# A two-layer transformer block on one core: which engine adds in the first pass, and who orders the second layer

## The chip, the cores and the metric

The kernel runs on one core of one Trainium2 chip. The metric is the device time of one execution in microseconds (us); the result is compared as the median of several runs. The core has a matrix engine (TensorE, in the profile PE; its weight loads are PEld), VectorE (DVE), ScalarE (ACT), GpSimd (POOL), and SyncE (SP), which here only starts transfers (DMA). Every engine works through a queue of its own, strictly in the queue's order; semaphores hold an instruction back until what it reads is there and what it overwrites is no longer needed. TensorE writes its products to PSUM; everything else lies in SBUF or in HBM.

## The reference

Two layers over x of shape 8 x 256 x 512 (2048 tokens, 512 channels), all in float32. In each layer the normalized tokens go to an attention and to a feed-forward part, and both results are added to x.

```
x  = hidden_states                                  # (8, 256, 512)
xn = layernorm(x)
# layer 0, attention: 32 heads of 128, linear attention with decay
qkv    = silu(xn @ qkv_w.T)                          # 512 -> 3 * 4096
attn   = causal (q k^T * decay) v, per head          # scanned in blocks of 32
normed = norm_w * attn * rsqrt(mean(attn^2) + eps)   # over 4096
L0a    = (sigmoid(xn @ gate_w.T) * normed) @ out_w.T # 4096 -> 512
# layer 0, feed-forward: 16 experts, 2 chosen per token, and a shared one
L0f    = sum_e gate_e * ((silu(xn@w1+b1) * (xn@w2+b2)) @ w3 + b3) + shared(xn)
x  = x + L0a + L0f
xn = layernorm(x)
# layer 1, attention: one head of 128, softmax over 256 tokens
L1a = softmax(q k^T / sqrt(128)) v @ Wo + bo
# layer 1, feed-forward: 64 low-rank experts of rank 16, 16 chosen per token
G   = softmax over the 16 best of xn @ Wr.T          # (tokens, 64)
L1f = 2 * ((xn @ A) * G) @ B                         # 512 -> 1024 -> 512
out = x + L1a + L1f
```

## The kernel before

The 2048 tokens are four chunks of 512 (`CH`), each chunk two sequences of 256 (`S`). The program has four stages. The opening (0 to about 134 us) normalizes, computes the router and the shared expert. Two passes over the heads follow: the first (134 to 1240 us) for chunks 0 and 1, the second (to about 2406 us) for chunks 2 and 3. The second layer comes last, chunk by chunk (2406 to 2688 us).

**Seven products for eight.** The large matrix products are done by a scheme that multiplies two 2 x 2 block matrices with seven products p1 to p7 of sums of blocks, in place of eight. In the passes it is applied twice, one inside the other: an *outer product* (class `Outer`, one of seven in `ORDER`) takes one weight operand and one token operand, and computes its own product by seven inner ones. A pass goes over 8 groups of four heads (`g`), two halves of each (`h` = 0: q and k; `h` = 1: gate and v), and seven outer products: 112 outer products, 784 inner ones.

One outer product runs so (the loop over `plan`, L1500): p1 into a bank `ps_a`, p7 into `ps_e`, then p3 of the outer product *before*, then p6 (into the same `ps_a`), p4 (`ps_e`), p2 (`ps_b`), p5 (`ps_a`). In between, a running sum in a bank is taken out three times (`copied`, L1218: c1 after p1, c3 after p7, c2 after p6), and four results for the four quarters `q` of a tile are made from a bank and such a copy (`result`, L1227). Two banks `ps_a`, one `ps_e`, one `ps_b` are all there is, so a later product into a bank waits until it is taken out.

The four tiles `a`, `b`, `c`, `d` (named `c` in the profile) collect the outer products: p1 gives a; p2 gives b = a + product; p5 gives c = a + product; p3 gives d = c + product; p6, p4 are added to a, p7 to a and c. There are two ways to add such a running tile: *folded* (L1214), when the copy out of the bank is itself an addition on VectorE, `cp<-ps_a,c`; or apart, when ScalarE copies (`cp<-ps_a`, L1224), VectorE adds the bank to it, and GpSimd adds the tile afterwards (`c<-c`, `c<-c,r`). Before, the second pass folds (`self.u.i` is 1) and the first does not (0). In p7, the second pass adds the fourth result from the bank to c and to a on VectorE; the first copies it with ScalarE and lets GpSimd add it to c and VectorE to a. VectorE also does the first pass's other additions `a <- a + r` of p7 (`add_a`).

**Weight operands** (`weights`, L839). In the second pass all sums of weight blocks come ready from HBM. The first pass makes them while the outer product before runs, and stores them (`store`, issued by ScalarE). `outer_sum` (L849) makes the operand of p6, p5, p3 and p7 from the raw quarters, on 2 x 256 columns at a time (`w<-w 128x512`); p6's step makes p5's too, so it has four of them, p3 and p7 two each, and the others none: eight in each half of a group. `inner_sum` (L852) makes the four sums for the inner products, w7 = w1 - w0, w4 = w0 + w3, w5 = w4 - w1 and w6 = w2 - w5 (`w<-w 128x256`); the last on GpSimd, the rest on VectorE. The list `steps` says after which inner product of the running outer product each is issued.

Between the inner products smaller pieces of work are issued (`later`, `slot`): `silu` and `gate` (ScalarE, L975 to L982), scores, `attend` (the square of `ps_o` on ScalarE, its sums on GpSimd, `gT` on VectorE, L1031), the output product L1084 with its addition `acc<-ps_sc,acc`, and in the second pass the experts. Near the end of each pass, `combine` (L643, seven additions of `acc` on GpSimd) and `finish` (L649, VectorE) turn the sums of the chunks into the layer's result.

**Order.** In the two passes the queues of ScalarE, GpSimd and VectorE stand in the order of issue (`tc.manual_schedule`, L811). TensorE's and SyncE's are ordered by a planner. In the opening and in the second layer the planner orders all of them, but for instructions marked `keep_in_program_order`.

**Second layer** (the loop at L1633). For each chunk: `low_rank(0)` and `low_rank(2)` multiply the tokens by A, with the seven products in `seven` (L1552): p1, p2, p6, p7, p5, p3, p4, the bank copied by ScalarE (L1558) or added up by VectorE (`cp<-ps_b`, `cp<-ps_e`) and multiplied by the gates (`hg<-cp,spread_g`); then a third `seven` multiplies by B, adding `cp` to the output on GpSimd and the bank on VectorE, and writes the rows out. Dictionaries `fill1`, `fill2` and `fill` say what is issued behind each product. For the chunk itself: `turned` (transposes of the softmax, a copy `pT`), `weighed` (times v), `attended` (times Wo; `bo` is added on GpSimd, `spare<-spare,wob`). For the chunk after it: `gather` (GpSimd's indirect transfers of the experts' rows), `settle` (adds them, L629), for chunks 2 and 3 `finish`, then `stats` and `scaled` (the layer norm, L256 and L263), and in the third `seven` the transposes (L283), `route` with `choose` (the gates of the 64 experts, L710 to L720), `qk`, `softmax` (L755 to L764) and `gates`, whose result goes to HBM (`gd<-GT`) and comes back spread over the partitions (`spread_g<-gd`). Chunks 2 and 3 have their `combine` issued here too (`steps`, L1779). Chunk 0's share of this is done at the end of the second pass.

Of the kernel before, what the change touches and what calls it, by code (L numbers as in the profile page):

```python
# [73 lines left out]
def block_kernel(  # L74
# [24 lines left out]
    nc = tc.nc  # L99
# [438 lines left out]
    at = NTT * E  # L538
# [110 lines left out]
    def finish(i, r, ns=range(TPC), kept=lambda ins: ins):  # L649

        for n in ns:
            o = r[:, n, :].rearrange("p (h c) -> p h c", h=2)
            at = 2 * (n // 2)
            kept(
                nc.vector.scalar_tensor_tensor(
                    o, acc[i][:, at : at + 2, n % 2], all_rms[i][:, n : n + 1], o, ALU.mult, ALU.add
                )
            )
# [152 lines left out]
    with tc.tile_pool(name="attn", bufs=1) as attn, tc.manual_schedule(engines={mybir.EngineType.Activation, mybir.EngineType.Pool, mybir.EngineType.DVE}):  # L811
# [27 lines left out]
        def weights(i, g, h, p, steps):  # L839

            w = loaded[p].pop(0)
            y = w[:, 0:4]
            v = nc.vector
            pool = nc.gpsimd
            kept = ws[2 * g + h][p]
            if i == 0:
                latest[p] = y

                def outer_sum(f, o, a, b, n):  # L849
                    f(o[:, n : n + 2], a[:, n : n + 2], b[:, n : n + 2], v)  # L850

                def inner_sum(f, o, a_, b_):  # L852
                    f(w[:, o], w[:, a_], w[:, b_], pool if o == 6 else v)
                    if o == 6:
                        later(6, store)

                def store():
                    nc.scalar.dma_start(out=kept, in_=w[:, 4 if p in RAW else 1 : 8])

                outer = []  # L860
                if p == "p6":
                    w5 = loaded["p5"][0]
                    outer = [(add, w5, w5, w5[:, 4:8]), (sub, y, w5, y)]
                elif p == "p3":
                    outer = [(sub, y, y, latest["p6"])]
                elif p == "p7":
                    outer = [(sub, y, y, w[:, 4:8])]
                for n, when in ((0, "p1"), (2, "p7")):
                    steps += [(when, partial(outer_sum, *at, n)) for at in outer]
                steps += [  # L870
                    (when, partial(inner_sum, *at)) for when, at in (
                        ("p7", (sub, 7, 1, 0)), ("p6", (add, 4, 0, 3)), ("p6", (sub, 5, 4, 1)), ("p2", (sub, 6, 2, 5))
                    )
                ]
            return dict(zip(("p1", "p2", "p4", "p5", "p6", "p3", "p7"), (w[:, n] for n in range(1, 8))))
# [316 lines left out]
        class Outer:  # L1192
# [20 lines left out]

            def folded(self, q):  # L1214

                return self.u.i and (self.p, q) not in (("p4", 0), ("p4", 3)) and {"p2": "a", "p5": "a", "p6": "a", "p4": "a", "p3": "c"}.get(self.p)

            def copied(self, bank, q):  # L1218
                c = attn.tile([P, 512], FP, tag="cp", name="cp", bufs=5)
# [7 lines left out]
            def result(self, i, j, bank, c):  # L1227

                u, p, q = self.u, self.p, 2 * i + j
                pool = nc.gpsimd  # L1230
                a = u.tile(self.h, "a")[:, q]
                made, with_ = dict(
                    p1=("a", None), p2=("b", "a"), p5=("c", "a"), p3=("d", "c")
                ).get(p, (None, None))
                if made:
                    o = u.tile(self.h, made)[:, q]
                    if c is None and with_ is None:
                        nc.scalar.copy(o, bank)
                    elif c is None:
                        add(o, bank, u.tile(self.h, with_)[:, q])  # L1240
                    else:
                        add(o, bank, c)
                        if with_ and not self.folded(q):
                            add(o, o, u.tile(self.h, with_)[:, q], pool)
                elif p != "p7" and (c is None or self.folded(q)):
                    add(a, bank, a if c is None else c)
                elif p == "p7" and c is None and u.i:
                    c_ = u.tile(self.h, "c")[:, q]
                    add(c_, bank, c_)
                    add(a, bank, a)  # L1250
                else:
                    r = attn.tile([P, 512], FP, tag="sum", name="r", bufs=4)
                    if c is None:
                        nc.scalar.copy(r, bank)
                    else:
                        add(r, bank, c)
                    if p != "p7":
                        add(a, a, r, pool)
                    else:
                        c_ = u.tile(self.h, "c")[:, q]  # L1260
                        add(c_, c_, r, pool)

                        self.added.append(partial(add_a, a, r, pool if u.i else nc.vector))
                        if (i, j) == (1, 1):
                            for n in range(3):
                                later(n, self.added.pop(0)) if n else self.added.pop(0)()
                        elif (i, j) == (0, 1):
                            self.added.pop(0)()
                whole = dict(p2=("b", 0, 0), p3=("d", 0, 1), p7=("c", 1, 1), p4=("a", 1, 0)).get(p)
                if whole and (i, j) == (0, 1):  # L1270
                    Part(u, self.h, whole[1], whole[2], u.tile(self.h, whole[0])).begin()
# [228 lines left out]
        for n, (i, g, h, p) in enumerate(plan):  # L1500
            cur = outers[n]
            u = cur.u
# [126 lines left out]
        return x_  # L1629


    out_t = out.rearrange("(i t p) c -> i t p c", t=TPC, p=P)
    for i in range(NCH):  # L1633
        xc, yT = accs[i], xT[i]
# [74 lines left out]
        following = []  # L1709
        if i + 1 < NCH:  # L1710
# [1 line left out]
            for n in range(TOP):  # L1712
                gather(i + 1, n, following[1 + n])
        fill1 = {
            1: [],
            2: [partial(turned, 0)], 7: [partial(turned, 1)], 5: [partial(weighed, 0)], 3: [partial(weighed, 1)], 4: [],
        }
        fill2 = {k: [partial(attended, t)] for t, k in enumerate((2, 7, 5, 3))}
        fill2[4] = []
        if following:  # L1720
            settled[i + 1] = spare()
            whole = Normal(settled[i + 1], following[0])

            def stats(t):
                whole.stats(t, tc.keep_in_program_order)

            def scaled(t):
                tc.keep_in_program_order(whole.scaled(t))

            if i:  # L1730
                fill1[1].append(lambda: finish(i + 1, following[0], kept=tc.keep_in_program_order))
            for n, fill, k, ts in (
                (0, fill1, 3, (0, 1)), (0, fill1, 4, (2, 3)), (1, fill2, 2, (0, 1)), (1, fill2, 7, (2, 3)),
            ):
                fill[k].append(partial(settle, i + 1, n, following[0], following[1 + n], ts))
            fill2[7] += [partial(stats, 0), partial(stats, 1)]
            fill2[5] += [partial(stats, 2), partial(stats, 3), whole.root]
            fill2[3] += [partial(scaled, 0), partial(scaled, 1)]
            fill2[4] += [partial(scaled, 2), partial(scaled, 3)]
# [136 lines left out]
```

## Time and profile before

| | us |
|---|---|
| median of 3 runs | 2686.19 (2685.26 to 2689.57) |
| the profiled execution's own time | 2689.79 |
| its span, first to last instruction | 2688.1 |

| stage (us) | PE busy | PEld | DVE | ACT | POOL |
|---|---|---|---|---|---|
| opening, 0 to 134 | 121.0 | 69.6 | 101.5 | 51.4 | 82.1 |
| first pass, 134 to 1240 | 1083.4 | 971.5 | 872.1 | 427.1 | 776.2 |
| second pass, 1240 to 2406 | 1159.7 | 1035.5 | 707.8 | 312.8 | 501.1 |
| second layer, 2406 to 2688 | 267.0 | 216.2 | 177.3 | 49.0 | 66.8 |

The mean granted clock of TensorE is 0.994 of full. The profile was taken from one execution. A busy time counts the union of an engine's instructions; the ends of matmuls are modelled, so a busy TensorE may still be slowed, which shows in the distance from one start to the next. In a group's line stand the source line, engine and operation, output and inputs by the program's names, shapes, and the number of instructions; then the busy time and the mean of one in ns; then the time that the engine stood idle just before them, and for what. Additions all have line L103, since one helper issues them: they are told apart by the names of their tiles. In a line of the waits stand who waited for whom, and then the total, the number of times and the longest.

### The profile page before, as it was taken

To read this page: it belongs to the slowest core of one execution; us is meant where nothing else is said; L and a number is where in the kernel's file an instruction comes from. 1 tells how busy PE (TensorE), PEld (TensorE's weight loads), DVE (VectorE), ACT (ScalarE), POOL (GpSimd) and SP (SyncE) were. 2 spreads that over 40 slices of the span, in tenths; PEclk is the share of its full clock that TensorE was granted. 3 is DMA by queue.
4 is the path that set the end of the run, shared out by engine and by line. 5 is a ranking of instruction groups with operands and counts; after the bars stand their busy time and mean duration, and the time that the engine had idled before them with its cause. 6 is when DMAs were issued, how large, how long until landed. Compare 5 with 4: busy or idle time off the path is not lost. (4 is left out here: it accounts for less than half of the span.)

```text
span 2688.1 us, 38735 instructions
## 1 busy us (share of the span) xinstructions
PE 2631.1 (98%) x14218; PEld 2292.8 (85%) x14218; DVE 1858.7 (69%) x3161; ACT 840.3 (31%) x1233; POOL 1426.1 (53%) x1326
## 2 busy tenths in 40 slices
PE   8999999999999999999999999999999999999999
PEld 5578888888888888888989898888989898977777
DVE  8698777778787878766556565656666565757763
ACT  4234343434343434342322123222313132321121
POOL 7458686868686767574433435353433454463210
PEclk8999999999999999999999999999999999999999
DMA  6798686868686868695868676777768686634211
GB/s 251 290 384 307 234 299 227 299 234 300 233 299 234 307 231 306 227 332 206 299 244 281 219 290 237 268 268 249 261 234 282 236 310 223 223 102 145 79 42 65
DMA packets 163120, 655.62 MB, mean 244 GB/s; under 512 B 19776, under 2 KB 22336, under 8 KB 160960
## 3 DMA queue, kind: packets, MB, share of 16 engines
q1 hardware_dynamic: 125936, 499.16, 52.7%
q10 hardware_dynamic: 21024, 92.81, 8.5%
q0 software_dynamic: 15968, 61.13, 6.8%
q8 instruction: 115, 1.88, 0.3%
q14 instruction: 77, 0.63, 0.1%
HBM read 512.13 MB, written 143.78 MB: 244 GB/s over the span
## 5 line engine op out<-in xcount | busy, mean ns | idle before, releaser
L887 PE MATMUL ps_a<-xt,w 128*128 128x256 f32 x2688 | 717.5, 382 | 8.4 <-ACT cp L1224 4.1
L887 PEld LDWEIGHTS ps_a<-xt,w 128*128 128x128 f32 x2688 | 470.7, 191 | 65.7 <-issue 11.2
L103 POOL TENSOR_TENSOR c<-c,r 128x512 f32<-128x512 f32 x288 | 382.1, 1346 | 217.2 <-DVE r L103 217.0
L1084 PE MATMUL ps_sc<-wo,gT 128*128 128x256 f32 x1792 | 424.0, 380 | 3.2 <-ACT head L758 2.6
L1224 ACT COPY cp<-ps_a 128x512 f32<-128x512 f32 x304 | 177.5, 584 | 678.5 <-PE ps_a L887 586.3
L1084 PEld LDWEIGHTS ps_sc<-wo,gT 128*128 128x128 f32 x1792 | 334.3, 190 | 47.8 <-issue 5.0
L887 PE MATMUL ps_e<-xt,w 128*128 128x256 f32 x1344 | 366.2, 381 | 7.0 <-DVE c L103 6.5
L103 DVE TENSOR_TENSOR w<-w 128x256 f32<-128x256 f32 (+1 forms) x464 | 353.8, 771 | 5.4
L103 POOL TENSOR_TENSOR sums<-sums,sq 128x256 f32<-128x256 f32 x240 | 192.4, 802 | 304.5 <-ACT sq L1022 294.9
L887 PEld LDWEIGHTS ps_a<-w,xt 128*128 128x128 f32 x1792 | 270.5, 191 | 23.0
L887 PE MATMUL ps_a<-w,xt 128*128 128x128 f32 x1792 | 272.3, 275 | 0.0
L103 POOL TENSOR_TENSOR c<-c 128x512 f32<-128x512 f32 x144 | 191.4, 1339 | 146.5 <-DVE c L103 138.1
L887 PEld LDWEIGHTS ps_e<-xt,w 128*128 128x128 f32 x1344 | 232.1, 191 | 31.6 <-DVE c L103 8.0
L103 DVE TENSOR_TENSOR acc<-ps_sc,acc 128x512 f32<-128x512 f32 x196 | 134.6, 688 | 149.2 <-PE ps_sc L1084 149.0
L1031 DVE SCALAR_TENSOR_TENSOR gT<-ps_o,nw,c 128x256 f32<-128x256 f32 x256 | 112.0, 479 | 166.0 <-ACT sq L1022 137.9
L103 DVE TENSOR_TENSOR c<-ps_a,c 128x512 f32<-128x512 f32 x192 | 130.3, 686 | 97.8 <-PE ps_a L887 97.0
L887 PE MATMUL ps_b<-xt,w 128*128 128x256 f32 x672 | 182.1, 380 | 0.0
L103 DVE TENSOR_TENSOR s<-ps_sc,decay 128x384 f32<-128x384 f32 x256 | 140.1, 553 | 56.3 <-PE ps_sc L999 55.4
L103 POOL TENSOR_TENSOR gT<-gT 128x512 f32<-128x512 f32 x128 | 170.2, 1330 | 5.5 <-DVE gT L1031 3.0
L1022 ACT ACTIVATE sq<-ps_o 128x512 f32<-128x512 f32 x128 | 76.6, 599 | 301.3 <-PE ps_o L1012 277.5
L1011 PE MATMUL ps_o<-s,c 128*128 128x256 f32 x512 | 157.3, 389 | 8.9 <-DVE gT L1031 8.5
L998 PE MATMUL ps_sc<-c 128*128 128x256 f32 x512 | 152.6, 380 | 0.0
(293 smaller groups left out, 4288.1 us busy)
## 6 DMA issues: line engine op xcount, KB each, us to landing
xt<-xc SPq DMA_DIRECT2D x224, 896.0 KB
w<-in_w_att_dram SPq DMA_DIRECT2D x144, 512.0 KB
w<-in_w_att_dram SPq DMA_DIRECT2D x48, 384.0 KB
wo<-in_w_out_dram SPq DMA_DIRECT2D x56, 256.0 KB
decay<-dec SPq DMA_DIRECT2D x32, 384.0 KB
yd<-ye SPq DMA_DIRECT2D x36, 256.0 KB
wos<-wo ACTq DMA_DIRECT2D x32, 256.0 KB
wo<-wos SPq DMA_DIRECT2D x32, 256.0 KB
```

Source lines behind the costliest of these rows:

```text
L103: (eng or nc.vector).tensor_tensor(o, a, b, op)
L887: mm(o, a, b, start=(first and ty == 0), stop=True, skip_group_check=True)
L998: mm(p[:, 0:S], k[:, 0:P], q, start=True, stop=True)
L1011: mm(po[:, bass.ts(hh, S)], v[:, 0:P], s[:, 0:S], start=True, stop=False)
L1022: nc.scalar.activation(sq, po, AF.Square)
L1031: nc.vector.scalar_tensor_tensor(gT[:, h, :], po[:, bass.ts(h, S)], nw[:, n : n + 1], self.c[:, 2 * h + t, 0:S], ALU.mult, ALU.mult,)
L1084: mm(py[:, bass.ts(t, S)], self.O[l, p][:, hh, bass.ts(t, P)], self.wo[p][:, hh, :], start=(t == 0 and hh == 0), stop=(hh == 1), skip_grou ...
L1224: nc.scalar.copy(c, bank)
```

## The change

In the first pass: `outer_sum` goes from VectorE to GpSimd; for the outer products that have one (p6, p3, p7), `inner_sum`s are issued later (w7 after p4 in place of p7, w4 and w5 after p2 in place of p6, w6 after p5 in place of p2). `folded` holds in the first pass as in the second, so that the running tile is added by VectorE in the copy out of the bank; the fourth result of p7 is added from the bank on VectorE; the other `add_a` go to GpSimd. What is computed stays the same.

In the second layer: ScalarE, GpSimd and VectorE work in the order of issue. Both `turned` come one product earlier or more (after p1 and p2 of the first `seven`, in place of p2 and p7), and `finish` of the following chunk is issued in two parts, after p2 and p7, in place of one after p1.

```diff
--- before.py
+++ after.py
@@ -847,7 +847,7 @@
                 latest[p] = y
 
                 def outer_sum(f, o, a, b, n):
-                    f(o[:, n : n + 2], a[:, n : n + 2], b[:, n : n + 2], v)
+                    f(o[:, n : n + 2], a[:, n : n + 2], b[:, n : n + 2], pool)
 
                 def inner_sum(f, o, a_, b_):
                     f(w[:, o], w[:, a_], w[:, b_], pool if o == 6 else v)
@@ -867,9 +867,10 @@
                     outer = [(sub, y, y, w[:, 4:8])]
                 for n, when in ((0, "p1"), (2, "p7")):
                     steps += [(when, partial(outer_sum, *at, n)) for at in outer]
+                whens = ("p4", "p2", "p2", "p5") if outer else ("p7", "p6", "p6", "p2")
                 steps += [
-                    (when, partial(inner_sum, *at)) for when, at in (
-                        ("p7", (sub, 7, 1, 0)), ("p6", (add, 4, 0, 3)), ("p6", (sub, 5, 4, 1)), ("p2", (sub, 6, 2, 5))
+                    (when, partial(inner_sum, *at)) for when, at in zip(
+                        whens, ((sub, 7, 1, 0), (add, 4, 0, 3), (sub, 5, 4, 1), (sub, 6, 2, 5))
                     )
                 ]
             return dict(zip(("p1", "p2", "p4", "p5", "p6", "p3", "p7"), (w[:, n] for n in range(1, 8))))
@@ -1213,7 +1214,7 @@
 
             def folded(self, q):
 
-                return self.u.i and (self.p, q) not in (("p4", 0), ("p4", 3)) and {"p2": "a", "p5": "a", "p6": "a", "p4": "a", "p3": "c"}.get(self.p)
+                return (self.p, q) not in (("p4", 0), ("p4", 3)) and {"p2": "a", "p5": "a", "p6": "a", "p4": "a", "p3": "c"}.get(self.p)
 
             def copied(self, bank, q):
                 c = attn.tile([P, 512], FP, tag="cp", name="cp", bufs=5)
@@ -1244,7 +1245,7 @@
                             add(o, o, u.tile(self.h, with_)[:, q], pool)
                 elif p != "p7" and (c is None or self.folded(q)):
                     add(a, bank, a if c is None else c)
-                elif p == "p7" and c is None and u.i:
+                elif p == "p7" and c is None:
                     c_ = u.tile(self.h, "c")[:, q]
                     add(c_, bank, c_)
                     add(a, bank, a)
@@ -1260,7 +1261,7 @@
                         c_ = u.tile(self.h, "c")[:, q]
                         add(c_, c_, r, pool)
 
-                        self.added.append(partial(add_a, a, r, pool if u.i else nc.vector))
+                        self.added.append(partial(add_a, a, r, pool))
                         if (i, j) == (1, 1):
                             for n in range(3):
                                 later(n, self.added.pop(0)) if n else self.added.pop(0)()
@@ -1629,6 +1630,7 @@
         return x_
 
 
+    ctx.enter_context(tc.manual_schedule(engines={mybir.EngineType.Activation, mybir.EngineType.Pool, mybir.EngineType.DVE}))
     out_t = out.rearrange("(i t p) c -> i t p c", t=TPC, p=P)
     for i in range(NCH):
         xc, yT = accs[i], xT[i]
@@ -1712,8 +1714,8 @@
             for n in range(TOP):
                 gather(i + 1, n, following[1 + n])
         fill1 = {
-            1: [],
-            2: [partial(turned, 0)], 7: [partial(turned, 1)], 5: [partial(weighed, 0)], 3: [partial(weighed, 1)], 4: [],
+            1: [partial(turned, 0)],
+            2: [partial(turned, 1)], 7: [], 5: [partial(weighed, 0)], 3: [partial(weighed, 1)], 4: [],
         }
         fill2 = {k: [partial(attended, t)] for t, k in enumerate((2, 7, 5, 3))}
         fill2[4] = []
@@ -1728,7 +1730,8 @@
                 tc.keep_in_program_order(whole.scaled(t))
 
             if i:
-                fill1[1].append(lambda: finish(i + 1, following[0], kept=tc.keep_in_program_order))
+                for k, ns in ((2, (0, 1)), (7, (2, 3))):
+                    fill1[k].append(lambda ns=ns: finish(i + 1, following[0], ns, tc.keep_in_program_order))
             for n, fill, k, ts in (
                 (0, fill1, 3, (0, 1)), (0, fill1, 4, (2, 3)), (1, fill2, 2, (0, 1)), (1, fill2, 7, (2, 3)),
             ):
```

## The prediction

> **What bounds the kernel now.** I read the page, then busy time by stretch, then TensorE's waits, the groups of the first pass, and two places of the timeline.
>
> ```profile
> span 2688.1 us, 38735 instructions
> ...
> PE 2631.1 (98%) x14218; PEld 2292.8 (85%) x14218; DVE 1858.7 (69%) x3161; ACT 840.3 (31%) x1233; POOL 1426.1 (53%) x1326
> ```
>
> TensorE is never idle for long, so only its idle 57 us and slow starts can be won. Where are they? First pass, second pass, second layer:
>
> ```profile
> 269.00:1210.00 941.00, 925.68 (x5109) 832.35 (x5109) 736.75 (x1132) 361.24 (x523) 672.44 (x609) 1.00 0.75 269
> 1277.00:2285.00 1008.00, 1005.87 (x5772) 900.09 (x5772) 599.16 (x971) 259.90 (x362) 416.19 (x407) 1.00 0.73 260
> 2352.00:2688.10 336.10, 316.89 (x1445) 256.58 (x1444) 207.54 (x464) 64.84 (x128) 100.51 (x85) 0.99 0.27 87
> ```
>
> The columns are length, then busy time of PE, PEld, DVE, ACT, POOL. Idle PE: 15.3, 2.1 and 19.2 us. Unhindered, a matmul of 256 columns starts 0.216 us after the one before, one of 128 after 0.110. Adding up every excess over such pitches from the starts in the timeline gives 31.5 us in the first pass, 10.5 in the second, 3.5 in the slice 202 to 269 before, and 22 from 2388 on, which 6.5 before 2406. The excess holds the idle time, slow restarts, and two stretches of 3.4 us at half clock (granted 0.97 in their slices: 1.7 us lost each).
>
> ```profile
> PE ps_o L1011 <- DVE gT L1031: 8.0, 7, 1.4
> PE ps_e L887 <- DVE c L103: 5.3, 7, 1.2
> PE ps_a L887 <- DVE r L103: 1.5, 4, 0.4
> PE ps_a L887 <- DVE c L103: 0.2, 1, 0.2
> ```
>
> All of the first pass's waits are for VectorE, which there is 78% busy (59% in the second pass). Its groups:
>
> ```profile
> L103 DVE TENSOR_TENSOR w<-w 128x256 f32<-128x256 f32 x285 | 193.9, 680 | 3.7
> L103 DVE TENSOR_TENSOR w<-w 128x512 f32<-128x512 f32 x108 | 105.5, 987 | 0.9
> L103 DVE TENSOR_TENSOR c<-c,r 128x512 f32<-128x512 f32 x56 | 68.2, 1246 | 0.0
> ...
> L103 DVE TENSOR_TENSOR c<-ps_e,cp 128x512 f32<-128x512 f32 x56 | 38.2, 681 | 0.2 <-PE ps_e L887 0.2
> ```
>
> An addition with an operand in PSUM costs 0.68 always. One wholly in SBUF costs 0.68 at its best too (0.41 with 256 columns), but 0.99 to 1.25 on average: it is what GpSimd's additions hold up. ScalarE's part in the waits:
>
> ```profile
> 652.40 1.06 ACT L980 ACTIVATE c<-c 128x1024 f32<-128x1024 f32 x1 [4.03 <-POOL c L103]
> 653.36 1.04 ACT L981 ACTIVATE c<-c 128x1024 f32<-128x1024 f32 x1
> 654.43 1.15 ACT L982 ACTIVATE c<-c,half 128x1024 f32<-128x1024 f32 x1
> ...
> 655.96 0.60 ACT L1022 ACTIVATE sq<-ps_o 128x512 f32<-128x512 f32 x1
> ```
>
> The gate waits 4 us for GpSimd's last `c` addition; the copies of `cp` and the square queue behind it, then `gT`, then TensorE's L1011 (1.4 us). And at the layers' seam:
>
> ```profile
> 2390.60 12.63 POOL L103 TENSOR_TENSOR acc<-acc 128x512 f32<-128x512 f32 x10
> ...
> 2395.70 2.50 DVE L764 TENSOR_SCALAR head<-head,stot 128x256 f32<-128x256 f32 x2
> ...
> 2400.63 1.97 PE L1084 MATMUL ps_sc<-wo,gT 128*128 128x256 f32 x8 [2.25 <-ACT head L758]
> 2400.76 2.62 DVE L764 TENSOR_SCALAR head<-head,stot 128x256 f32<-128x256 f32 x2
> ```
>
> Ten `combine` additions keep GpSimd busy without a break; the pair L764, 0.60 us at 2551.74, takes 2.5.
>
> **First pass, counts.** Counted in the built programs: VectorE gains 240 PSUM additions (240 x 0.686 = +165 us), loses 128 outer weight sums (x 0.986 = -126) and 64 additions `c<-c,r` (x 1.248 = -80): -41. ScalarE loses 224 copies (x 0.584 = -131). GpSimd loses 144 `c<-c` (x 1.339) and 32 `c<-c,r` (x 1.346) and gains the 128 outer sums, which it never did: bounded by its own 512-column additions, 1.25 undisturbed to 1.77 held up; I take 1.33, the mean of the same form: -66.
>
> **What that does on TensorE's path.** The second pass runs the same folding already, and loses 10.5 us in 1008, or 9.8 over 941. That is the floor of the first pass's loss. Its VectorE has no weight sums, though; after the change the first pass's is still some 75% busy, and now three copies per outer product, done by ScalarE so far, stand in its queue. The test is the short outer products: of 98 in the first pass, 28 follow each other within 6.5 us (seven products of 0.86, nothing between). VectorE must do in each seven PSUM additions (0.60 from start to start) and three weight sums (0.40): 5.4 of 6.05 us. It fits while the sums meet no GpSimd addition. Between an outer product's `outer_sum` on GpSimd and its `inner_sum` on VectorE the new `whens` put the time from p1 to p4, so they rarely meet. p6's four sums take GpSimd 4 x 1.33 = 5.3 us, and w4 is wanted at p2, five products or 4.3 us after p1; but GpSimd's queue has little ahead of them there and starts early, so I cost that wait at nothing (1 us each, 16 times, if that cover is missing). In p7's outer product GpSimd has six additions instead of four; p4's `cp<-ps_a,c` waits for the fourth of them. The second pass has that wait: 3.0 us over all, none reaching TensorE. The gate's `c` now comes from VectorE for quarter 1 and ahead of the `a` additions for quarter 3, which shortens the 41 us that ScalarE waits for `c`.
> Loss left: from 9.8 (the second pass's) to twice that, as VectorE is fuller; I take 13. Gain 31.5 - 13 = 18, and 2 more in the slice before it: -20, bounds -12 to -24.
>
> **Layers' seam.** Under order of issue the last 14 `combine` additions (i = 2, 3) move into the second layer's iterations 0 and 1. With GpSimd quiet, L756 and L764 shrink by 1.0 + 1.9 + 0.4 + 2.0, and the waits of 0.3, 2.3 and 1.4 us on TensorE go: -4 (bounds -5, 0).
>
> **Second layer proper, 15.6 us of excess.** Gains: `scaled` 0 and 1 now come ahead of the last `cp`, and `hs` behind 2 and 3, so the transposes' waits (2.3, 1.3 and with `yT` 3.4 us) shrink by perhaps 5. The sync queue issues `gd` ahead of two output rows, 2.3 us of issue, and in iteration 1 the gates' first half ahead of the 1 MB load of `xr`. Costs: the seven `combine` additions now run while VectorE makes `hs` and `hg` (1.2 us each, 2.29 beside GpSimd's run at 2590): +2 in two iterations. `finish` (four of 0.73) used to fill VectorE's wait for `spread_g`; now it stands behind that wait, and behind it `cp<-ps_e`, which p4 needs: I count +0.9 in iteration 2, and in iteration 1 the wait of 1.5 stays. There GpSimd's four additions of `bo` can also meet `hg` (a run of five of these held one for 7.0 us at 2416): 0 to +3.5. Sum -5 + 4 + 1 + 1 = about +1; bounds -6 (gains alone, and 1 from the gates) to +8 (6 + 0.9 + 3.5 against gains of 2).
> Moved at no cost: the eight gathers of each following tile now stand on GpSimd behind `combine` and the last `spare<-cp`; at 1.3 us each they are issued within some 9 us of the end of p4 (2479 in iteration 1), and `settle` asks for them at 2497. `turned` brings its transposes (0.4 us of TensorE each) and copies forward into p1 and p2, where their inputs are ready. The four `choose` run one after another, each waiting half a microsecond for ScalarE's `es`, about 9 us in all, with the copy `c2` behind the `es` on ScalarE; p6, p7 and the 6.9 us of `qk` stand before TensorE wants that bank, and VectorE idles 8.7 us there now. The weight stores go three slots later on ScalarE, while their buffer is kept by p3's product anyway.
>
> The Trainium skill (SBUF — State Buffer, Who interferes with whom) says that a VectorE instruction with two SBUF inputs is shut out for the whole of a GpSimd instruction that reads SBUF, and that PSUM inputs keep it free. The rows agree for single additions, but at 2416 VectorE lost to five in a row. By the page the 336 sums left on VectorE would each risk one addition of GpSimd, which speaks against giving GpSimd more; by the rows GpSimd gets 66 us less to do in all.
>
> Sum, against this execution's own 2689.8 (span 2688.1): 2689.8 - 20 - 4 + 1 = 2667. The median of the runs is 3.6 lower, 2686.2: **2663.5**. Own range 2650 to 2676: the first pass's bounds with some of the second layer's.
>
> **Rivals.**
> *VectorE becomes the bound in the short outer products.* For it: three evacuations more in its queue, 0.6 us of room. If GpSimd's additions meet two of three weight sums at their 90th percentile (1.37, so +0.95 each), 7.3 us are wanted in 6.05: 1.25 x 32 (28 of 98, for all 112) = 40 us lost. With the forecast's 24 of gains kept: 2686 + 40 - 24 = 2702. It decides from 24 / 32 = 0.75 us per short product on. Against it: the second pass runs four such products at 6.05 without loss, and GpSimd has less to do.
> *The waits only change their name.* `gT` waits 70 us for the square in either pass, and evacuations now stand behind it; half the first pass's loss stays (-10), the second layer gives +6: 2678.
> *The new order in layer two eats everything:* its bound of +8, `hg` shut out for 4 us in each of three iterations (+12), and only -12 in the first pass: 2686 - 12 - 4 + 20 = 2690, no change.
>
> **How the numbers follow.** Forecast 0.55 (2650 to 2676); names change 0.17 (2676 to 2684); no change 0.12; VectorE-bound 0.16. A measurement tells 0.2%, 5.4 us: faster is below 2680.8. That takes the forecast and two thirds of the second: 0.66; same 0.16 (the rest of the second and the third's 0.10); slower 0.18. The range reaches from 2650 to 2692: above lies most of the slower case.
>
> **What would show it.** After: no `w<-w` of 512 columns on DVE, its 256s near 0.45 us; idle PE in the first pass near 5 us with no `PE ps_e <- DVE c`; L980's wait for POOL under 20 us; L764 at the seam 0.6 the pair. Wrong if DVE waits for POOL `w`, if PE waits for `DVE cp` in the first pass by more than 15 us, or if the second layer's 336 us grow by over 8.

## The result: no gain, and the profile after

| | us |
|---|---|
| before, median of 8 runs | 2685.80 (2683.49 to 2689.57) |
| changed, median of 8 runs | 2693.66 (2687.04 to 2695.81) |
| ratio, with its 95% interval | 1.0023 (1.0012 to 1.0034) |
| predicted | 2663.5, range 2650 to 2692 |

The changed kernel is some 0.2% slower, and the prediction of a gain was wrong. Its page (busy time per engine), and then busy time in the stretches that the prediction used (length, then PE, PEld, DVE, ACT, POOL, granted clock, DMA share, GB/s):

```profile
span 2688.9 us, 38358 instructions
...
PE 2632.3 (98%) x14218; PEld 2294.4 (85%) x14218; DVE 1785.8 (66%) x3209; ACT 712.7 (27%) x1009; POOL 1306.1 (49%) x1278
```

```profile
269.00:1210.00 941.00, 936.03 (x5201) 844.97 (x5200) 688.13 (x1194) 254.64 (x334) 572.35 (x571) 1.00 0.75 271
1277.00:2285.00 1008.00, 1004.43 (x5739) 897.77 (x5738) 597.18 (x969) 261.65 (x365) 421.87 (x412) 1.00 0.72 257
2352.00:2688.90 336.90, 309.99 (x1356) 247.82 (x1354) 201.49 (x451) 58.60 (x120) 90.56 (x74) 0.96 0.25 81
```

VectorE, ScalarE and GpSimd work 73, 128 and 120 us less than before. TensorE's idle time in the first pass falls from 15.3 to 5.0 us, as forecast. In the last stretch it rises from 19.2 to 26.9 us, and the clock there falls from 0.99 to 0.96: what the first pass won, the second layer lost.

These windows are fixed in time, so they don't hold quite the same work before and after. A table by work shows it more sharply. For each matmul I take the excess of the distance to the next start over the unhindered distance (0.216 us for 256 columns, and so on, as in the prediction), and cut the execution where the same amount of work is done, at what was 134, 269, 1210, 2352, 2405, 2478 and 2552 us before. Excess in us:

| kernel | 134 to 269 | to 1210 | to 2352 | seam, to 2405 | layer two, to 2478 | to 2552 | to the end |
|---|---|---|---|---|---|---|---|
| before | 12.4 | 31.5 | 13.0 | 7.0 | 7.3 | 3.5 | 5.0 |
| changed | 14.5 | 12.7 | 14.5 | 2.2 | 10.1 | 16.9 | 9.4 |

The stretch from 269 to 1210 us -18.8, seam -4.8, second layer +20.6 (15.8 to 36.4), the rest +3.6. (The sum is near nothing: the profiled executions took 2689.8 and 2690.6 us. The one before lies 4.0 above its median of 8 runs, the other 3.1 below, so about 7 of the medians' 7.9 us are between executions, and no profile here shows them.) Of the 18.8, some 3.4 us are the two stretches of half clock that the profile before has there: the kernel e2 below, whose first pass is that of before, has neither, and the same count reads some 3.5 us less for it. The seam's part is visible in one line, the pair that took 2.5 us before:

```profile
2382.39 0.62 DVE L764 TENSOR_SCALAR head<-head,stot 128x256 f32<-128x256 f32 x2
```

TensorE's waits in the first pass (269 to 1210 us), and in the second layer (2384 to 2688 us), changed kernel:

```profile
PE ps_e L888 <- PE ps_a L888: 3.0, 7, 0.4
PE ps_a L888 <- DVE c L103: 1.9, 4, 0.5
```

```profile
PE ps_o L1698 <- DVE pT L1686: 8.7, 2, 6.2
PE ps_e L1663 <- DVE cp L103: 3.8, 4, 1.3
PE ps_sc L283 <- DVE spare L263: 3.2, 3, 1.5
PE ps_a L1762 <- DVE hs L103: 2.0, 1, 2.0
PE ps_sc L682 <- DVE yT L288: 1.5, 1, 1.5
```

The waits for `gT` and for `c` in `ps_e` are gone from the first. In the second the largest is new: the second `weighed` product waits 6.2 us in iteration 1 and 2.5 in iteration 2 for the second `pT`. The timeline of the first of these (start, duration, engine, line):

```profile
2464.16 0.99 POOL L618 DMA_INDIRECT spare<-yd,slots  x1 [0.30 <-issue]
...
2464.55 0.51 SPq L774 DMA_DIRECT2D gd<-GT  x1
...
2468.89 3.14 SPq L786 DMA_DIRECT2D spread_g<-gd  x4
...
2470.94 4.94 POOL L103 TENSOR_TENSOR spare<-spare,wob 128x512 f32<-128x512 f32 x4
...
2479.97 0.69 DVE L103 TENSOR_TENSOR hg<-cp,spread_g 128x512 f32<-128x512 f32 x1 [10.73 <-DMA spread_g<-gd]
2480.58 0.68 DVE L1686 COPY pT<-ps_sc 128x512 f32<-128x512 f32 x1
2481.18 2.73 DVE L655 SCALAR_TENSOR_TENSOR x<-acc,rms,x 128x512 f32<-128x512 f32 x4
...
2481.32 2.08 PE L1698 MATMUL ps_o<-pT,v 128*128 128x256 f32 x4 [6.20 <-DVE pT L1686]
...
2483.83 0.69 DVE L103 TENSOR_TENSOR cp<-ps_e,cp 128x512 f32<-128x512 f32 x1
```

VectorE stands still for 10.7 us at the first `hg`, since its gates have not landed; behind it in the queue stand `pT`, the `finish` of 2.7 us and `cp<-ps_e`, and for the first and the last of these TensorE waits. The same place before:

```profile
2481.93 0.51 SPq L774 DMA_DIRECT2D gd<-GT  x1
...
2484.29 2.47 SPq L786 DMA_DIRECT2D spread_g<-gd  x4
2492.64 0.69 DVE L103 TENSOR_TENSOR hg<-cp,spread_g 128x512 f32<-128x512 f32 x1 [4.76 <-DMA spread_g<-gd]
```

There the gates' reload starts 2.4 us after `gd` is issued, and `hg` follows 10.7 us after it; now 4.3 and 15.4. In iteration 2 it was 2.4 and 8.1, and is 4.2 and 11.8. And the stop costs more than its own length. Busy time and clock (the last figures but two) of the stop and of the 10 us behind it:

```profile
2476.00:2481.00 5.00, 0.00 (x0) 0.00 (x0) 1.03 (x2) 0.00 (x0) 0.00 (x0) 0.83 0.79 213
2481.00:2491.00 10.00, 8.51 (x23) 6.44 (x24) 8.71 (x14) 0.78 (x2) 0.00 (x0) 0.57 0.25 95
```

TensorE restarts at half clock: 6.4 us of excess from the stop, and 4.9 more before the clock comes back, 1.2 of them idle in front of p4, which waits for `cp<-ps_e`.

What else moved there are the transfers. The queues in the 18 us from `gd`'s issue on (packets, MB, share of the 16 engines), changed and then before:

```profile
q1 hardware_dynamic: 1022, 2.54, 47.3%
q0 software_dynamic: 528, 1.70, 35.0%
```

```profile
q1 hardware_dynamic: 1060, 2.76, 48.5%
```

Queue q0 is GpSimd's: the gathers of the next chunk. Before, the planner had issued them at 2433 to 2451 and at 2507 to 2527 us, when no gates were awaited; in the order of issue they stand where the gates are loaded.

### The profile page after: what moved, and what is told of

It is laid out like the page before. It is cut to its first block, busy times and chain, and to the rows that moved or that the text cites. A ratio compares the mean times of both kernels' runs of the same rounds, so it can differ in the third digit from the quotient of the medians.

```text
span 2688.9 us, 38358 instructions
## 1 busy us (share of the span) xinstructions
PE 2632.3 (98%) x14218; PEld 2294.4 (85%) x14218; DVE 1785.8 (66%) x3209; ACT 712.7 (27%) x1009; POOL 1306.1 (49%) x1278
## 5 line engine op out<-in xcount | busy, mean ns | idle before, releaser
L103 POOL TENSOR_TENSOR c<-c,r 128x512 f32<-128x512 f32 x256 | 322.8, 1283 | 243.6 <-DVE r L103 243.4
L103 POOL TENSOR_TENSOR w<-w 128x512 f32<-128x512 f32 (+1 forms) x240 | 242.2, 1019 | 220.8 <-DVE w L103 181.7
L103 POOL TENSOR_TENSOR sums<-sums,sq 128x256 f32<-128x256 f32 x240 | 179.3, 747 | 337.9 <-ACT sq L1023 327.7
L103 DVE TENSOR_TENSOR cp<-ps_a,c 128x512 f32<-128x512 f32 x288 | 198.1, 688 | 60.5 <-PE ps_a L888 48.9
L1225 ACT COPY cp<-ps_a 128x512 f32<-128x512 f32 x160 | 93.5, 585 | 534.2 <-PE ps_a L888 503.5
L103 DVE TENSOR_TENSOR c<-ps_a,c 128x512 f32<-128x512 f32 x224 | 151.0, 685 | 78.3 <-PE ps_a L888 77.4
L103 DVE TENSOR_TENSOR w<-w 128x256 f32<-128x256 f32 x336 | 184.3, 549 | 17.6 <-POOL w L103 13.8
```

The source lines that it names most:

```text
L103: (eng or nc.vector).tensor_tensor(o, a, b, op)
L1225: nc.scalar.copy(c, bank)
```

## The experiments

Three theories for the second layer: *queue* (in the order of issue `pT` and `finish` stand behind `hg`), *collision* (the gathers hold up `gd` and `spread_g` on the DMA engines), *GpSimd* (its runs of additions hold VectorE). Each time is a median; the ratio is to the kernel before, run beside it.

**The halves alone.** The changed kernel without its second-layer part, and that part on the kernel before.

> The first pass's edits alone; the second layer as before (planned order, turning and finishing where they were). If the loss lies in the second layer: the stretch from 134 to 1210 us keeps its 16 us of gain (43.9 to 27.5 us of excess on TensorE), the seam keeps its old waits of 4 us and the second layer its old 16 us of excess: some 2669 us, 0.994 of before. If the second layer's loss in the changed kernel came from what the first pass left behind (its shorter time, another clock, a seam that comes earlier), the second layer is slow here too: 2685 or more.

> The second layer's edits alone; first pass as before. Theory: the seam gains 3 us and the second layer loses 18.5 (15.6 to 34 us of excess), so some 2701 us, 1.006 of before, with waits of weighed (L1698) for DVE pT near 6 and 2.5 us and stretches of half clock behind them. Rival (the loss needs both parts): 2683 to 2690.

First pass alone (e1): 2676.41 us, 0.9958 (0.9944 to 0.9973). Second layer alone: 2706.59 us, 1.0071 (1.0057 to 1.0086). The loss belongs to the second layer's edits, whose excess there is 36.1 us without the first pass's, too. The two differences, -10.9 and +19.3, add up to +8.4 us, against +7.9 for both together. But the first pass's edits alone bring 11 us, not 20: 269 to 1210 us gains its 18.8, while 134 to 269 loses 4.2, and one wait at 2200 us grows from 1.3 to 3.2 us, which with 1.7 us lost to the half clock behind it makes 3.6 more.

**Turning ahead.** Both turnings issued before the first `hg`:

```diff
-            1: [partial(turned, 0)],
-            2: [partial(turned, 1)], 7: [], 5: [partial(weighed, 0)], 3: [partial(weighed, 1)], 4: [],
+            1: [partial(turned, 0), partial(turned, 1)],
+            2: [], 7: [], 5: [partial(weighed, 0)], 3: [partial(weighed, 1)], 4: [],
```

> The changed kernel, with the second half's turning (pT of b = 1) taken ahead of the first hg product in VectorE's queue. Queue theory (pT behind hg is what stops TensorE): the waits of 6.2 and 2.6 us at L1698 and most of the half clock behind them go, -10 to -14 us against the changed kernel, some 2681. Rival (hg itself is late, for its gates land late, and cp<-ps_e stands behind it as well): the same wait reappears at p4 of the first product, named after DVE cp, and the time falls by 1 to 3 us only, some 2691.

2694.28 us, 1.0022 (1.0014 to 1.0031), as the changed kernel. The wait for `pT` is gone and this one, of the second layer's waits, stands in its place:

```profile
PE ps_e L1663 <- DVE cp L103: 12.5, 3, 7.7
```

The rival holds: `pT` was only the first in the row behind `hg`. The name of a wait is not its cause.

**Gathers held back.** A one-column copy on GpSimd that reads the gates makes the gathers wait until these have landed (and `settle` comes two slots later, to fit):

```diff
-            for n in range(TOP):
-                gather(i + 1, n, following[1 + n])
...
+                if j == 0 and following:
+                    nc.gpsimd.tensor_copy(following[1][:, 0, 0:1], gates2[1][:, 1, 0:1])
+                    for n in range(TOP):
+                        gather(i + 1, n, following[1 + n])
```

> The changed kernel, with the gathers of the next tile held back until the gates (spread_g of the second half) have landed, and settle moved two slots later to fit. Collision theory (the gathers, 2.1 MB, share the DMA engines with gd and spread_g): the first hg comes 10.7 and 8.2 us after the issue of gd, as before, in place of 15.4 and 11.8 in the changed kernel; TensorE's stop in front of p4 shrinks by 4.7 and 3.6 us and the half clock behind it shrinks too: -8 to -14 us, some 2682. Queue theory: hg may come sooner, but the finishing of 2.7 us and pT still stand between, -2 to -4 us at most. Rival (the output rows or the load of xr are what delays the gates): hg stays 15 and 11 us behind gd, and the time stays within 2 us of the changed kernel.

`hg` now follows `gd` by 7.9 and 8.3 us, and the wait for `cp<-ps_e` at p4 is 1.0 and 1.4 us: the collision is real. (Before, in iteration 1, the 1 MB load of `xr` stood in front of the reload, and `hg` came after 10.7 us; e4 has the changed kernel's order on SyncE, with the load behind, and against it `hg` comes 7.6 and 3.6 us later in the changed kernel.) The time is 2693.41 us, 1.0016 (1.0006 to 1.0027), no better, for now the gathers land late: in iteration 1 `settle` waits 2.3 and 4.3 us for them, and is then held by GpSimd's run of `bo` additions, 6.0 us where one takes 0.75.

```profile
2489.80 6.02 DVE L629 SCALAR_TENSOR_TENSOR x<-spare,slot_gates,x 128x512 f32<-128x512 f32 x1 [4.30 <-DMA spare<-yd,slots]
2490.31 4.94 POOL L103 TENSOR_TENSOR spare<-spare,wob 128x512 f32<-128x512 f32 x4
```

The second layer's largest waits:

```profile
PE ps_e L1667 <- DVE cp L103: 12.5, 4, 5.2
PE ps_sc L1712 <- DVE spare L103: 3.5, 1, 3.5
```

**Gathers ahead, and bo on VectorE: two by two.** The gathers of a chunk issued in the iteration before (`ahead`), after p2 and p5 of its third seven; and, apart from it, `attended`'s additions of `bo` on VectorE:

```diff
+            def ahead(n, early=early):
+                early.append(spare())
+                gather(i + 2, n, early[n])
+
+            fill[2].append(partial(ahead, 0))
+            fill[5].append(partial(ahead, 1))
```

```diff
-            add(xc[:, t, :], xc[:, t, :], bo_t, nc.gpsimd)
+            add(xc[:, t, :], xc[:, t, :], bo_t)
```

> The changed kernel, with the gathers of a tile issued one iteration earlier (in the third seven of the iteration before, after p2 and p5), so that none is under way when gd and spread_g are loaded, and none later than settle asks. Collision theory: the first hg 8 to 11 us behind gd instead of 15.4 and 11.8; the stops in front of p4 of 8 and 4.5 us (with the half clock 11.3 and 6.8) fall by half, and nothing new waits: -8 to -12 us, some 2683. Queue theory (order alone costs the loss): no more than -3, some 2691.

> The changed kernel with the bo additions on VectorE and nothing else. If the stop of 6.2 us in front of the second weighed product is the gates' landing (the gathers on the DMA engines) and not GpSimd's run of additions, the first hg still comes 15 and 11 to 12 us behind gd and the time stays within 4 us of the changed kernel, 2690 to 2696. If it is GpSimd's run, it falls by 8 to 14.

> The kernel with the gathers an iteration ahead, and the four bo additions of an iteration (attended) on VectorE instead of GpSimd. Theory (GpSimd's run of six additions held the second L764 for 7.2 us, and with it ts, p6 and the turning): that hold falls to 0.6 us, the waits of 4.3 and 1.4 us at the turning go in both iterations with the half clock of 6.8 us behind each: -12 to -18 us against that kernel, some 2672. Rival (what moves to VectorE, 0.69 us for each of 16, is late in its own queue): -5 at most.

| | bo on GpSimd | bo on VectorE |
|---|---|---|
| gathers as changed | 2693.66; excess 36.4 | 2695.83, 1.0035 (1.0023 to 1.0047); 36.4 |
| gathers ahead | 2686.55, 1.0000 (0.9991 to 1.0009); 28.4 | 2676.96, 0.9967 (0.9955 to 0.9979); 19.3 |

(Excess in us in the second layer; 15.8 before.) With `bo` alone moved nothing is gained, and `hg` still comes 12.5 and 12.8 us behind `gd`: the stop is not GpSimd's run. With the gathers ahead as well `hg` comes after 9.5 and 9.0 us and no stretch of half clock is left in the second layer; its largest waits:

```profile
PE ps_sc L283 <- DVE spare L263: 4.8, 4, 1.9
PE ps_e L1664 <- DVE cp L103: 3.3, 3, 1.8
PE ps_b L1764 <- DVE hg L103: 2.6, 3, 1.0
```

So the gathers' place costs 17 us of excess with `bo` on VectorE (36.4 to 19.3), and 8 with `bo` on GpSimd. The 17 include the wait of 2 us for `hs` and its half clock: the gathers also stand between the `combine` additions on GpSimd now, and break up their run. With the gathers ahead but `bo` on GpSimd (e5) a new stop eats half the gain. Its timeline:

```profile
2466.06 7.20 DVE L764 TENSOR_SCALAR pb<-pb,stot 128x256 f32<-128x256 f32 x2
2466.31 0.51 SPq L774 DMA_DIRECT2D gd<-GT  x1
...
2466.71 1.27 POOL L103 TENSOR_TENSOR spare<-cp,spare 128x512 f32<-128x512 f32 x1
...
2467.94 4.91 POOL L103 TENSOR_TENSOR spare<-spare,wob 128x512 f32<-128x512 f32 x4
...
2473.14 1.09 PE L1683 MATMUL ps_sc<-ident,pb 128*128 128x128 f32 x4 [4.15 <-DVE pb L764]
...
2474.79 2.48 SPq L786 DMA_DIRECT2D spread_g<-gd  x4
...
2479.74 0.69 DVE L103 TENSOR_TENSOR hg<-cp,spread_g 128x512 f32<-128x512 f32 x1 [2.15 <-DMA spread_g<-gd]
```

A pair of 0.6 us is held until GpSimd has done its last addition. In the changed kernel that run fell where VectorE waited for the gates anyway. So `hg` comes 13.4 and 14.7 us behind `gd` here, and not the 8 to 11 expected: SyncE issues the reload only 8.5 us after `gd`, behind two output rows that VectorE makes after this stop. From the reload's issue to `hg` it is 5.0 and 6.2 us, against 11.1 and 7.6 in the changed kernel, as the collision theory has it.

**Combine later.** Its seven additions after p5 (five) and p4 (two) of the third seven, not after p2, p7, p5 and p3.

> The changed kernel, with the seven combine additions of the third seven placed after p5 (five) and after p4 (two) instead of after p2, p7, p5 and p3. Theory (GpSimd's run of four holds VectorE's hs and hg, 2.3 us each for 1.2): TensorE's waits for hs and yT in the third seven (2.1 and 1.6 us, with half clock behind them 4.9 and 3.2) go: -4 to -7 us, some 2688. Rival (they meet the softmax's L764 or the ts subtractions there instead): within 2 us of the changed kernel.

2689.72 us, 1.0015 (1.0006 to 1.0024): the waits for `hs` and `yT` are gone as expected, but the stop at L1698 in iteration 2 grew from 2.5 to 5.9 us, so second-layer excess falls only to 33.0 and the gain is unclear.

**Everything mended in the order of issue.** Gathers ahead, `combine` later, both turnings ahead, `finish` after p5, the first `hg` product behind `cp<-ps_e`; then, on top, the first half of the first group (`g` = 0, `h` = 0, the "half unit" below) unfolded; and the former with `bo` on VectorE and both gathers after p2.

> The changed kernel with four edits of the second layer: gathers an iteration ahead, combine after p5 and p4, both turnings ahead of the first hg, finish after p5, and that first hg product itself taken behind cp<-ps_e, so that p4 doesn't wait for the gates. If these are the whole loss, the second layer's excess on TensorE falls from 34 us to some 12 and the time to some 2671, faster than before. If something else costs the rest (the order of issue as such), it stays above 2680.

> The kernel with these edits, and the first half unit (i = 0, g = 0, h = 0) unfolded as it was, ScalarE copying there. If the loss of 4 to 6 us in the stretch 134 to 202 us came of the folded additions queueing behind the routing's work on VectorE, that stretch goes from some 14 us of excess to some 9: -4 to -5 us against the kernel with the layer edits alone, some 2667. Rival (the outer sums on GpSimd hold the routing's additions): the stretch stays at 13 or more.

> The kernel with the four mended places of the second layer, the bo additions on VectorE and both gathers ahead already after p2. There a run of nine additions on GpSimd held ts for 7.2 us and p6 for 9.7 in two iterations, with half clock of 10.2 us behind each. If GpSimd's runs are what costs it, both stops go: -24 to -28 us, some 2665, faster than the first-pass edits alone (2676). Rival (something else of the order of issue costs as much): 2676 or more.

2690.74 us, 1.0018 (1.0009 to 1.0027); 2695.16, 1.0034 (1.0022 to 1.0046); 2681.20, 0.9981 (0.9972 to 0.9989). All three missed the time that was hoped for. In the first two GpSimd's run holds `ts`:

```profile
2463.83 7.20 DVE L103 TENSOR_TENSOR ts<-yT 128x512 f32<-128x512 f32 x1
...
2465.57 4.91 POOL L103 TENSOR_TENSOR spare<-spare,wob 128x512 f32<-128x512 f32 x4
...
2471.90 1.62 PE L1664 MATMUL ps_a<-ts,fa 128*128 128x256 f32 x3 [9.60 <-DVE ts L103]
```

With that run gone the third still has 22.8 us of excess; its largest waits are for `cp<-ps_e` (7.0 us in four) and for L764 (3.1 us in two), and what holds these was not followed further. With the first half unit unfolded, 134 to 269 us reads 19.4 us, the most of all kernels.

**Planned second layer.** The first-pass edits alone with `bo` on VectorE (e12); with the first half unit's outer sums back on VectorE as well (e13); with most of GpSimd's `low` additions (sums of the second layer's weights, made in the second pass) two to four slots later on top (e14); with `combine` of the last two chunks on VectorE on top of that (e17). Beside them, as e14 but the second layer's GpSimd alone in order of issue, gathers ahead and `combine` later (e15), and the first-pass edits with all outer sums on VectorE (e16).

> The first-pass edits alone, second layer in planned order, bo additions on VectorE. In planned order the runs of bo additions held hg (6 to 7 us) where TensorE had other work: the waits left there are 1.3 to 2 us each, so -1 to -4 us, some 2674. If the planned order gains as much as the order of issue does from it, 2668 or less.

> The first-pass edits with planned second layer and bo on VectorE; in the first half unit (g = 0, h = 0) the outer sums stay on VectorE as before. If these sums on GpSimd hold the routing's additions (3.7 us for four of 64 columns at 144 us, 0.6 before) and with them TensorE, the stretch 134 to 202 us falls from 13.6 us of excess to about 9: -4 us against 2670, some 2666. If the folded additions are the cause, it stays at 13 or more.

> As the kernel before, with the low additions of fb (GpSimd, which wait up to 8.6 us for their load with six c additions behind them) put four slots later. If that wait is what grows the stop at 2200 us, the slice 2150 to 2218 falls from 5 us of excess to 2: another -3 us, some 2663. If not, the stop stays at 3 us or comes elsewhere.

> As the kernel with the low additions later (2668.6 us), with the 14 combine additions of the last two tiles on VectorE (0.69 us each) instead of GpSimd. Theory (GpSimd's run of ten at the seam holds L756 and L764): the waits for head L758 (0.3, 2.2) and acc (1.4) go and the slice 2352 to 2419 falls from 8.7 us of excess to 5: some 2664. Rival (VectorE's own queue at the seam is what is late; 14 more instructions make it later): 2668 or more.

> The kernel with both start and low mended, and in the second layer GpSimd alone in order of issue (VectorE and ScalarE planned), gathers an iteration ahead and after p2, combine after p5 and p4, bo on VectorE, turning and finishing as before the change. Theory (the loss was collision and GpSimd's runs, and the seam's gain comes of combine leaving the seam): seam 5 us of excess in place of 8.8, second layer 9 to 12: some 2660 to 2664. Rival (order of issue on any engine costs it): 2668 or more.

> The first-pass edits alone with the outer sums on VectorE throughout: folding and the additions to c on GpSimd or from PSUM remain. If folding alone brings the gain, 269 to 1210 us stays near 13 us of excess and the time near 2672; if VectorE needs the relief of the 128 sums (126 us) to take the folded additions, the short outer products become VectorE-bound: 269 to 1210 us rises to 25 or more, and the time to 2685 or more.

| kernel | us | ratio to before | 134 to 269 | to 1210 | to 2352 | seam | layer two |
|---|---|---|---|---|---|---|---|
| e1 | 2676.41 | 0.9958 (0.9944 to 0.9973) | 16.6 | 12.7 | 16.7 | 7.0 | 16.3 |
| e12 | 2670.35 | 0.9940 (0.9927 to 0.9953) | 15.2 | 12.6 | 16.0 | 7.9 | 10.6 |
| e13 | 2673.17 | 0.9945 (0.9932 to 0.9958) | 13.7 | 12.7 | 17.3 | 7.9 | 10.7 |
| e14 | 2668.61 | 0.9928 (0.9916 to 0.9941) | 14.6 | 12.8 | 16.4 | 7.0 | 8.7 |
| e17 | 2667.58 | 0.9927 (0.9913 to 0.9941) | 11.2 | 12.7 | 16.2 | 2.9 | 13.5 |
| e15 | 2677.98 | 0.9966 (0.9953 to 0.9978) | 14.7 | 12.7 | 16.3 | 2.2 | 23.0 |
| e16 | 2679.09 | 0.9967 (0.9954 to 0.9980) | 14.3 | 18.3 | 14.0 | 7.0 | 14.3 |

- Planned, the second layer has 10.6 us of excess where the order of issue, with the same `bo` and the gathers ahead, has 19.3. e12 to e14 and e17 beat both kernels; among these four the intervals overlap. e12 gained more than was expected (2674); e13 and e14 missed theirs (2666 and 2663).
- e17: without `combine` on GpSimd the seam's waits go (7.0 to 2.9), so GpSimd's run was their cause; the layer behind it gives as much back (8.7 to 13.5), so the time hardly moves.
- e15 missed by 14 us: with GpSimd alone in order of issue, the planner set `finish`, which waits for GpSimd's `acc`, ahead of the softmax's L764 on VectorE, and TensorE waits 1.9 and 2.5 us there in two iterations.
- e16: folding alone gives 13.2 of the 18.8 us, the sums' move the rest. In the time over all its interval overlaps with e1's, so there the sums' move is not clear of the noise. VectorE did not become the bound even with both.
- The loss in the start (134 to 269 us) stays open. e13 did not change it beyond the spread: kernels with the same code up to there read from 9.9 to 16.6 us in that stretch.
- The wait at 2200 us was still 2.8 us in e14, but e14 is no test of its theory: GpSimd waits 7.2 us for the load of `low` there, and 8.1 in e12, with a run of five additions `c<-c,r` behind it, and six in e12. What the runs do show: the wait is 1.1 to 1.3 us in the three kernels whose outer sums are all on VectorE (before, e2, e16) and 1.8 to 4.1 in the sixteen others. So it goes with the sums' move; by what way is open, for in e16 GpSimd waits 6.6 us for that load too, with six additions behind it.

## Why the prediction was wrong

**Right.** *First pass, bounds -12 to -24, taken at -20.* The stretch 269 to 1210 us lost 12.7 us of excess where I took 13, of 31.5 (some 28 without the half clock that e2 has not). The 2 us more "in the slice before it" did not come: 134 to 269 us lost 2.1. The signs named: no wait for `c` in `ps_e`; idle TensorE "near 5 us", measured 5.0; no outer sum on VectorE; the gate waits for GpSimd no more (but 66 us for VectorE's `c`, in place of 41, which costs TensorE nothing). GpSimd does one in 1.27 us (1.33 taken), and the 256-column sums cost VectorE 0.56 (0.45 forecast, 0.68 before):

```profile
L103 DVE TENSOR_TENSOR w<-w 128x256 f32<-128x256 f32 x288 | 159.9, 555 | 15.9 <-POOL w L103 12.6
L103 POOL TENSOR_TENSOR w<-w 128x512 f32<-128x512 f32 x110 | 139.1, 1272 | 2.3
```

VectorE does wait for GpSimd's sums, 12.6 us in all, which I had called a sign against me; none of it reaches TensorE. *Seam, -4:* measured -4.8, L764 0.62 us the pair as forecast, and the cause confirmed by e17.

**Wrong, and decisive.** *Second layer, "about +1; bounds -6 ... to +8":* measured +20.6, outside its bounds. The step that failed is this one: "Moved at no cost: the eight gathers of each following tile". I checked their place in GpSimd's queue and the time by which `settle` asks for them, and not whose transfers they run beside. They share the DMA engines with `gd` and `spread_g`, and the gates land 4.7 and 3.7 us later. The Trainium skill (DMA: Bandwidth & Descriptors, Queues, rings and completion order) says that each DMA engine takes packets in turn from every queue that has work for it; the later landing beside 528 packets of q0, and the earlier one once the gathers are held back (e4: 7.9 and 8.3 us behind `gd`), agree with that. (A small slip beside it: eight gathers "at 1.3 us each" are 10.4 us and not "some 9"; they took 10.7.)

Two further terms made of 4.7 us a loss of 11. *"`finish` ... now stands behind that wait, and behind it `cp<-ps_e` ...: I count +0.9 in iteration 2, and in iteration 1 the wait of 1.5 stays":* I had the queue right but priced it with the gates landing as before, and left out that the second `pT` stands in it too (e3 shows that its place alone is worth nothing). In iteration 1 p4 starts 20.0 us after `gd`, before 12.1: 4.7 of these 8 us come from the gates, 3.3 from `finish` (2.73) and `pT` (0.60). *The half clock:* my sum for the second layer has no term for it. Behind a stop of 6.4 us came 4.9 more, some 3.7 of them by the half clock.

*`bo`, "0 to +3.5" where it meets `hg`:* the mechanism was right and hidden in the changed kernel (e10: no gain); it is worth some 10 us (2686.55 to 2676.96) once the gathers are out of the way. *`combine`, +2 in two iterations:* the waits for `hs` and `yT` were 2.0 and 1.5 us, in one iteration each, and half clock of 3.4 us behind the first cost 1.7 more.

**Of the rivals**, the third came nearest: no change, "new order in layer two eats everything". Its place was right (`hg` late, three iterations at 4 us), its cause, GpSimd shutting out `hg`, was not: it was the landing of the gates. VectorE never became the bound. And without any loss in the second layer the time would still have been some 2673 (2693.7 - 20.6), not 2662.5 (2663.5 without its +1): 3.6 us are lost in the start and between 1210 and 2352 us, at 2200 us above all, whose causes stay open, and 6.7 lie in the executions: I set the profiled one 3.6 us above the median, as before, and it came out 3.1 below.

## What to carry to other kernels

When an order is changed by hand, list the transfers that move, each with its bytes, and ask which other transfer, on which someone waits, is under way at that time; their place in the issuing queue did not tell it here. A wait behind a late instruction was not cured by moving the instruction that bore its name (e3): the next in that queue took its place. Where a part that wins and a part that loses come in one change, measure them alone: here the first pass's edits with the second layer left to its planner give 2676 us, and 2668 to 2673 with `bo` off GpSimd.

## What the runs showed of the hardware

- A VectorE instruction with its operands in SBUF does not slip in between GpSimd's additions: pairs of 0.6 us or single ones of 0.69 were held 7.2 us by six additions in a row (with `bo` on GpSimd and the gathers ahead). The Trainium skill (SBUF — State Buffer, Who interferes with whom) says that the second comer is blocked for the whole instruction of the other engine; the runs show the hold to last over the whole run of instructions.
- After a stop TensorE's granted clock was half for 3.4, 6.8 or 10.2 us, multiples of 3.413 (the last of a trace is cut short by its end), and part of that can lie within the stop. It was 10.2 us around stops of 9.6 us (four times), and 6.8 or 10.2 around stops of 4.9 to 7.7. Stops of some 2 to 4.3 us were followed by 3.4 or 6.8 us, or by none (2.6 us at 2201 in the changed kernel). The Trainium skill (TensorE: Matmul & The Clock Gate, What's actually happening) explains the step by a free-running activity window of about 3.4 us; that up to three of them can follow one stop is what these runs add.
- Eight gathers of 0.26 MB, issued beside the gates' small store and reload, delayed the reload's start by 1.8 to 2.0 us and the first product with it by 3.7 to 4.7 us against the kernel before, and by 3.6 to 7.6 us against e4, which has the same order on SyncE.
